# The delta projections of a selective scan, issued in pairs in the two row halves of TensorE

## The chip, the cores and the metric

The kernel runs on one core of a Trainium2 chip, as one launch. The metric is the device time of the whole launch in microseconds, lower is better. It was 7049.78 us in the median of three runs (7040.85 to 7054.37) before the change. All data is 32-bit floating point.

## What is computed

Two layers on an input of 2 images of 48 x 48 tokens with 768 channels, each added to its input:

```python
x = x + neighbourhood_attention(group_norm(x))     # 12 heads of 64, 7x7 neighbourhood
x = x + bidirectional_mamba(group_norm(x))
```

The second layer is where the change lies. For each image and each of two directions (the second on the reversed sequence, with weights of its own), over L = 2304 tokens and 1536 inner channels with 16 states:

```python
xz = in_proj(x);  u, z = split(xz)
u = silu(causal_depthwise_conv4(u))
dt, B, C = split(x_proj(u), [48, 16, 16])
delta = softplus(dt @ dt_proj_w.T + dt_proj_b)     # contraction over 48 (49 with the bias row)
h[t] = exp(delta[t] * A) * h[t-1] + delta[t] * u[t] * B[t]      # per channel and state
y[t] = sum over states of h[t] * C[t]  +  D * u[t]
out = out_proj((y_forward + y_backward) * silu(z))
```

The change touches the line that makes `delta`.

## The kernel before

**Tiling of the scan.** A direction of an image is cut into 6 chunks of 384 tokens (`CL`, `CHUNKS`), and the 1536 channels into 12 tiles of 128. One *unit* is one channel tile of one chunk; there are 2 x 2 x 6 x 12 = 288 of them, in a fixed order. For a unit, `scan` works in 4 groups of 4 states: `hb` is filled with `delta * u * B` (line 1254, on VectorE or GpSimd, whichever the planner picks for groups 1 to 3), ScalarE makes the decays `da = exp(delta * A)` (line 1276, one instruction per state), VectorE scans two states at a time (line 1287), GpSimd multiplies by `C` (line 1302), and TensorE adds the states up by transposing each 128-token piece into the accumulator `py` (line 1319). ScalarE then copies `py` out (line 1345). There are 7 `hb` buffers.

**Deltas.** `deltas_of` makes the deltas of three units (`KB = 3`, called a triple here) in one go, one triple ahead of the scan; 96 triples in all. SP fetches `u` (line 1166) and the 49 x 384 piece of the projection's weights and bias `dtw` (line 1167). For each of the three channel tiles, TensorE does one matmul of 49 rows by 128 columns by 384 tokens into an accumulator `mm` (line 1180), and ScalarE copies it into `dlt` (line 1186). One softplus over all three tiles follows, with an activation table load before and after it (lines 1191 and 1192). GpSimd then multiplies `u` by the delta (line 1204). The right-hand side `dt`, 49 x 384 with a row of ones, is fetched once per chunk (line 1399). A 32-bit matmul shows as two weight loads and two MATMUL records in the trace.

**Accumulators.** The tag `mm` has two buffers of one PSUM bank each. They serve nearly everything besides the scan's own `py` and `du`: the delta projections, the input, gate, state and output projections (all at line 387), the second image's attention, and the transposes that add the two directions (line 1372). `dtw`, `u` and `dlt` have two buffers each.

**Order of the work.** Nothing is issued where it is written down. Every piece of work is entered into `Order` with an engine, a price in ns, a key (the unit at which it is wanted) and the buffers it reads and writes. `Order.run` then simulates the engines with these prices and writes out one fixed sequence, in which each engine keeps its order. At each step it takes the work that can start first; among works of one engine that could start within 150 ns, the one with the smaller key (less a bonus, `early`). A work can only be taken when each buffer that it needs is free, which means that all works of the buffer's former holder have been placed. Works of the kind `job` (the projections and attention of later stages) may run at most 2.5 units ahead of the oldest unfinished work of the scan. Where TensorE would have more than 800 ns without work during a scan, transposes of the identity (line 1520) are put in as filler.

**Stages.** Up to about 1000 us the first image's attention runs alone. From then on the scan of the 288 units runs through to the end, and beside it, as jobs: the first image's projections, then (about 2750 to 3600 us) the second image's attention, then that image's projections and the output projections.

The change is in `deltas_of` (lines 1162 to 1188) and `chunk` (lines 1396 to 1401). The pricing functions are `mm(n, cl) = n * (cl * 1.69 + 5)` ns for n matmuls of cl columns, multiplied by 1.05 during the scan, and `act(n) = 60 + 0.833 n` ns.

Of the kernel before, what the change touches and what calls it, by code (L numbers as in the profile page):

```python
# [16 lines left out]
P = 128  # L17
# [23 lines left out]
NS = 16  # L41
RK = 48
XD = RK + 2 * NS
CL = 384
CHUNKS = [(l, CL) for l in range(0, L, CL)]
NCH = len(CHUNKS)
# [3 lines left out]
KB = 3  # L50
EARLY = 20
# [199 lines left out]
def tile_kernel(  # L251
# [3 lines left out]
    nc = tc.nc  # L255
# [14 lines left out]
    for i, (conv_w, conv_b, xpT, dtT, dt_b, A_log, Dp) in enumerate((fwd, bwd)):  # L270
        q = {"dtT": dram.tile([RK + 1, DI], F32, tag=f"dtT{i}", name=f"dtT{i}")}
# [17 lines left out]

    ones = wk.tile([1, CL], F32, tag="yt", name="ones", bufs=1)  # L290
    nc.gpsimd.memset(ones, 1.0)
# [12 lines left out]
    us = [spill(t, [DI, L], ND * NCW) for t in ("uf", "ub")]  # L304
    xd = [spill(t, [XD + 1, L], NCW) for t in ("xdf", "xdb")]
    sz = spill("sz", [DI, L], ND * NCW)
# [6 lines left out]
    def cols(l0, cl, k0=0, nk=1):  # L313

        c0, c1 = l0 // CW, (l0 + cl) // CW
        return [k * NCW + c for k in range(k0, k0 + nk) for c in range(c0, c1)]
# [7 lines left out]
    def sb(tag, shape, n, parts=1):  # L324
        return Buf(f"{tag}_{n}", wk, shape, tag, BUFS.get(tag, 1), parts)

    def ps(tag, n):
        return Buf(f"{tag}_{n}", psum, [P, 512], tag, BUFS.get(tag, 1))
# [5 lines left out]
    def add(eng, ns, fn, key, r=(), w=(), job=False, size=0, after=None, early=0, alt=None, due=False, opens=None):  # L334

        news = [x[0] if isinstance(x, tuple) else x for x in w]

        def issue():
            for v in news:
                if v.ap is None:  # L340
                    v.ap = v.pool.tile(v.shape, F32, tag=v.tag, name=v.name, bufs=v.bufs)
            fn()

        if eng == "PE":

            ns *= 1.04 if key < 0 else 1.05
        return order.add(eng, ns, issue, key, r, w, job, size, after, early, alt, due, opens)

    def mm(n, cl):
        return n * (cl * 1.69 + 5)  # L350

    def act(n, pointers=0):
        return 60 + 90 * pointers + n * 0.833
# [180 lines left out]
    def attention(b, start, end, job, T):  # L534
# [16 lines left out]
        def tag(what, i):  # L551
            return T[what][i % len(T[what])]
# [93 lines left out]
        def core(t):  # L646
# [12 lines left out]
            for g in range(NP // PG):  # L659
# [4 lines left out]
                kv = "v" not in T  # L664
                here = (2 * KB * CL - nk) // (PG * P) if kv else 0
                ks = sb(tag("k", g), [P, nk + here * PG * P], f"k{n}", parts=1 + here)
# [242 lines left out]
    def in_proj(b, i, start, end, conv=True, gate=True, nk=KB, tags=("uz",), banks=("mm",), proj=None):  # L909
# [3 lines left out]
        lo, n = l0 - HALO, cl + 2 * HALO  # L913
        xc = sb("xc", [P, NC, CL + 2 * HALO], f"{b}_{i}_{conv:d}{gate:d}", parts=NC)
        a, z = max(lo, 0), min(lo + n, L)
# [90 lines left out]
        for x, k0 in enumerate(range(0, ND, nk)):  # L1006
            if conv:
                uz = sb(tags[x % len(tags)], [P, 2, nk, CL], f"u{b}_{i}_{k0}", 2 * nk)
                for kk in range(nk):
# [6 lines left out]
            if gate and x % 2:  # L1016
                uz = sb(tags[x % len(tags)], [P, 1, 2 * nk, CL], f"z{b}_{i}_{k0}", 2 * nk)
                for kk in range(2 * nk):
# [3 lines left out]
    def staged(src, l0, cl, n, key, w=None, wsrc=None):  # L1022
# [3 lines left out]
        def fetch():  # L1026
# [5 lines left out]
            "SP", 800 if w else 400, fetch, key - 0.5, r=[(src, cols(l0, cl, 0, ND))],  # L1032
            w=[s, w] if w else [s], job=True, size=ND * P * (cl + (XD if w else 0)) * 4,
        )
        return s

    def x_proj_of(b, back, i, acc, key):

        n, (l0, cl) = f"{b}_{back}_{i}", CHUNKS[i]
        w = sb("xpw", [P, ND, XD], n)  # L1040
        add(
            "SP", 400, lambda: nc.sync.dma_start(w.ap, par[back]["xpT"]), key, w=[w], job=True,
            size=P * ND * XD * 4,
        )

        def take(uz, k0, nk, key):
            def part():
                for kk in range(nk):
                    nc.tensor.matmul(
                        acc[:XD, :cl], w[:, k0 + kk, :], uz[:, back, kk, :cl], start=k0 + kk == 0,  # L1050
                        stop=k0 + kk == ND - 1,
# [9 lines left out]
    def xd_out(b, back, l0, cl, n, acc, key):  # L1061
        t = sb("ev", [P, TB], n)
        add(
            "ACT", act(cl), lambda: nc.scalar.copy(t[:XD, :cl], acc[:XD, :cl]), key + 0.05, r=[acc],
            w=[t], job=True,
# [91 lines left out]
    def deltas_of(ch, k0, x):  # L1157

        q, b, back, l0, cl, dt = (ch[v] for v in ("q", "b", "back", "l0", "cl", "dt"))
        c, h, at, n = slice(0, cl), slice(1, cl + 1), x - 1.0, f"{ch['s']}_{k0}"  # L1160

        u, w = sb("u", [P, KB, CL + 2], n, KB), sb("dtw", [RK + 1, KB * P], n)
        dl = sb("dlt", [P, KB, CL], n, KB)

        def fetch():
            nc.sync.dma_start(u[:, :, h], rows_of(us[back][b], k0, KB, l0, cl))
            nc.sync.dma_start(w.ap, q["dtT"][:, k0 * P : (k0 + KB) * P])

        add(
            "SP", 800, fetch, at - 0.7, r=[(us[back][b], cols(l0, cl, k0, KB))], w=[u, w],  # L1170
            size=P * KB * (cl + RK) * 4,
        )
        add(
            "ACT", 100, lambda: nc.scalar.copy(u[:, :, :: cl + 1], one), at - 0.3, w=[u], early=EARLY,
        )
        for j in range(KB):
            acc = ps("mm", f"dl_{n}_{j}")
            add(
                "PE", mm(1, cl),
                lambda j=j, acc=acc: nc.tensor.matmul(  # L1180
                    acc[:, c], w[:, j * P : (j + 1) * P], dt[:, c], start=True, stop=True
                ),
                at + 0.01 * j, r=[dt, w, u], w=[acc, (dl, j)], early=EARLY,
            )
            add(
                "ACT", act(cl), lambda j=j, acc=acc: nc.scalar.copy(dl[:, j, c], acc[:, c]),  # L1186
                at + 0.01 * j, [acc], [(dl, j)], early=EARLY,
            )

        def softplus():  # L1190
            nc.scalar.activation(dl[:, :, c], dl[:, :, c], AF.Softplus)  # L1191
            nc.scalar.preload_act_table_set("natural_log_exp_and_others")  # L1192

        add("ACT", 2600 + 120 + act(KB * cl), softplus, at + 0.05, [dl], [dl], early=EARLY)
        vts = [sb("vt", [P, CL], f"{n}_{j}") for j in range(KB)]
        for j in range(KB):
            add(
                "ACT", act(cl, 1) + 40,
                lambda j=j: nc.scalar.mul(vts[j][:, c], u[:, j, h], q["Dp"][:, k0 + j : k0 + j + 1]),
                at + 0.03 + 0.25 * j, [(u, j)], [vts[j]], early=EARLY,  # L1200
            )
            add(
                "POOL", 960,
                lambda j=j: nc.gpsimd.tensor_mul(u[:, j, h], dl[:, j, c], u[:, j, h]), at + 0.06 + 0.25 * j,  # L1204
                [(dl, j), (u, j)], [(u, j)], early=EARLY,
            )
        return [((dl, j), (u, j), vts[j]) for j in range(KB)]
# [184 lines left out]
    def chunk(b, back, i, at):  # L1392

        l0, cl = CHUNKS[i]
        s = f"{b}_{back}_{i}"
        dt = sb("dt", [RK + 1, CL], s)
        src = xd[back][b]
        add(
            "SP", 400, lambda: nc.sync.dma_start(dt[:, :cl], src[: RK + 1, l0 : l0 + cl]), at - 1.4,
            [(src, cols(l0, cl))], [dt], size=RK * cl * 4,  # L1400
        )
        bc = []
        for g in (0, 1, 2, NSG, 3, NSG + 1, NSG + 2, NSG + 3):

            o = int(g < NSG)
            t = sb(f"bc{g}", [P, SG, CL + 2 * o], s, 1 + o)
            r = RK + 1 + g * SG
            add(
                "SP", 400,
                lambda t=t, r=r, o=o: nc.sync.dma_start(  # L1410
                    t[:, :, o : o + cl], src[r : r + SG, l0 : l0 + cl].partition_broadcast(P)
                ),
                at - 1 + 0.25 * (g % NSG) + 0.3 * (g >= NSG), [(src, cols(l0, cl))], [t],
                size=P * SG * cl * 4,
            )
            bc.append((g, t))
        bc = [t for g, t in sorted(bc, key=lambda x: x[0])]
        ends = (0, NCH - 1)

        ys = ()  # L1420
        if (b, back, i) == passes[-1]:
            parts = [sb(tag, [P, n, CL], f"y{tag}{n}", n) for tag, n in (("uz", 2 * KB), ("uz", KB), ("u", KB))]
            ys = [(y, k) for y in parts for k in range(y.parts)]
        return dict(
            q=par[back], b=b, back=back, l0=l0, cl=cl, dt=dt, bc=bc, s=s, i=i, ys=ys,
            first=i == ends[back], final=i == ends[not back],
        )
# [29 lines left out]
    for b in range(nb):  # L1457
        f = b * 2 * NCH * ND
        if b:
            attention(b, *A1, True, BESIDE)  # L1460
        for i in range(NCH):
            start = P1 + 12 * i if b else 9 * (i - 1) - 4
# [7 lines left out]
            else:  # L1470
                take, last = x_proj_of(b, 0, i, das[0], start - 1)
                in_proj(
                    b, i, start, end, gate=False, nk=2, tags=HEAD, banks=("mm", "mm", "py", "du"),
# [31 lines left out]
    for x, (p, b, back, i, k) in enumerate(units):  # L1505
# [6 lines left out]
        elif back and k == ND - 1:  # L1512
            for h, (l0, cl) in enumerate(PIECES[i]):
                at = x + 2.5 + 5 * h if b else 188 + 2 * (2 * (NCH - 1 - i) + h)
# [56 lines left out]
```

## Time and profile before

| | us |
|---|---|
| median of three runs | 7049.78 |
| the profiled execution | 7040.0 |
| its span, first to last instruction | 7038.2 |
| TensorE busy, matmuls (40140 records) | 6280.1 |
| VectorE busy | 5990.5 |
| GpSimd busy | 5468.5 |
| ScalarE busy | 4851.3 |

The groups of instructions that carry the scan and the deltas (count, total busy us, mean ns of one):

| line, engine, what | count | busy | mean |
|---|---|---|---|
| 1287 VectorE scan of two states | 2304 | 3923.6 | 1749 |
| 1302 GpSimd product with C | 1152 | 3652.7 | 3186 |
| 1276 ScalarE decay of one state | 4608 | 2677.4 | 584 |
| 1319 TensorE transposes into `py` | 13824 | 1750.0 | 279 |
| 1254 GpSimd filling of `hb` | 502 | 1606.8 | 3203 |
| 1254 VectorE filling of `hb` | 650 | 1131.3 | 1746 |
| 1186 ScalarE copy of a delta tile | 288 | 133.4 | 475 |
| 1180 TensorE weight loads of the deltas | 576 | 91.8 | 188 |

The time of one execution comes from the hardware profiler. Busy time is the union of an engine's instructions. The ends of TensorE's instructions are modelled and overlap the next ones, so for TensorE the distance between starts says more than the duration. A line of the page such as "DVE 1343..." gives the busy share of 40 equal slices of the span in tenths. After the bar, a group's line gives its total busy time, the mean of one in ns, the idle time of its engine just before it, and what ended that idle time.

### The profile page before, as it was taken

Reading aid. Unit: us, or ns where it says so; the run is one execution under the profiler, and the core shown is the slowest. Engines: PE = TensorE matmul, PEld = TensorE weight load, DVE = VectorE, ACT = ScalarE, POOL = GpSimd, SP = SyncE. Lnnn points to the kernel's source line nnn. Section 1 sums busy time; section 2 is a strip of 40 time slices with the busy share of each in tenths; the row PEclk is TensorE's granted clock in tenths of the full one; section 3 lists DMA queues with packets and bytes.
Section 4 is the critical chain, followed back from the end, with each engine's and each line's share of the span. In section 5 each row is a group of like instructions: output and inputs, shape, how many; then the busy total and the mean of one; then the engine's idle time right before and its main releaser. Section 6 shows DMA issues by size and latency. Waiting matters only on the chain. (4 is left out here: it accounts for less than half of the span.)

```text
span 7038.2 us, 108877 instructions
## 1 busy us (share of the span) xinstructions
PE 6280.1 (89%) x40140; PEld 4878.2 (69%) x40140; DVE 5990.5 (85%) x6102; ACT 4851.3 (69%) x10516; POOL 5468.5 (78%) x1958
## 2 busy tenths in 40 slices
PE   8999899899899989899988888888888898999888
PEld 5666656666667767666766666666678887777777
DVE  1343459999999989878899999999999999999998
ACT  1222248878887777677877777788876667777774
POOL 0000019898889989777889999999999999999997
PEclk9999999999999999999999999999999999999999
DMA  6666454544565455555542443343466676655553
GB/s 194 185 214 190 143 174 131 153 137 133 162 190 162 148 165 166 161 175 155 179 152 87 137 138 89 95 143 114 139 179 191 175 218 198 192 176 160 163 171 104
DMA packets 1348293, 1115.48 MB, mean 158 GB/s; under 512 B 137840, under 2 KB 1338000, under 8 KB 1347728
## 3 DMA queue, kind: packets, MB, share of 16 engines
q1 hardware_dynamic: 1347760, 1108.50, 52.6%
q8 instruction: 318, 5.21, 0.3%
q14 instruction: 215, 1.76, 0.1%
HBM read 895.34 MB, written 213.57 MB: 158 GB/s over the span
## 5 line engine op out<-in xcount | busy, mean ns | idle before, releaser
L1287 DVE TENSOR_TENSOR_SCAN hb<-da,hb 128x772 f32<-128x772 f32 x2304 | 3923.6, 1749 | 200.1 <-ACT da L1276 148.8
L1302 POOL TENSOR_TENSOR hb<-hb,bc 128x1536 f32<-128x1536 f32 x1152 | 3652.7, 3186 | 379.4 <-DVE hb L1287 287.9
L1276 ACT ACTIVATE da<-dlt,A 128x384 f32<-128x384 f32 x4608 | 2677.4, 584 | 962.5 <-DVE hb L1287 884.9
L1319 PE MATMUL py<-ident,hb 128*128 128x128 f32 x13824 | 1750.0, 279 | 313.5 <-POOL hb L1302 306.6
L1319 PEld LDWEIGHTS py<-ident,hb 128*128 128x128 f32 x13824 | 1566.1, 143 | 570.5 <-POOL hb L1302 471.7
L1254 POOL TENSOR_TENSOR hb<-u,bc 128x1544 f32<-128x1544 f32 x502 | 1606.8, 3203 | 48.7 <-PE py L1319 42.6
L1254 DVE TENSOR_TENSOR hb<-du,bc 128x1544 f32<-128x1544 f32 x650 | 1131.3, 1746 | 37.3 <-ACT du L1231 27.5
L1204 POOL TENSOR_TENSOR u<-dlt,u 128x384 f32<-128x384 f32 x288 | 263.6, 917 | 478.0 <-ACT dlt L1191 386.9
L1520 PE MATMUL py<-ident 128*128 128x128 f32 x5124 | 630.8, 277 | 0.0
L387 PE MATMUL mm_xin<-xc,w_x 128*128 128x390 f32 x1656 | 592.6, 501 | 29.8 <-DVE uz_u L964 12.6
L387 PE MATMUL mm_z<-xc,w_z 128*128 128x384 f32 x1728 | 607.6, 492 | 6.3 <-ACT dlt L1186 3.8
L1520 PEld LDWEIGHTS py<-ident 128*128 128x128 f32 x5124 | 586.8, 143 | 17.3 <-issue 13.6
L387 PE MATMUL mm_out<-stage_y,w_o 128*128 128x192 f32 x3168 | 558.0, 330 | 18.9 <-DMA w_o<-in_w_opT 6.5
L387 PEld LDWEIGHTS mm_out<-stage_y,w_o 128*128 128x128 f32 x3168 | 519.0, 193 | 30.5 <-ACT dlt L1186 10.6
L930 POOL MEMSET xc<- 128x18 f32 x4 | 0.5, 118 | 630.0 <-PE mm_v L387 630.0
L964 DVE SCALAR_TENSOR_TENSOR uz_u<-mm_xin,conv_w,uz_u 128x384 f32<-128x384 f32 x792 | 427.9, 610 | 45.6 <-ACT uz_u L957 44.0
L387 PEld LDWEIGHTS mm_xin<-xc,w_x 128*128 128x128 f32 x1656 | 306.3, 193 | 230.2 <-issue 28.8
L387 PE MATMUL mm_qk<-xc_xn,w_qk 128*128 128x384 f32 x1296 | 452.8, 495 | 8.7 <-DVE sm L794 2.6
L387 PEld LDWEIGHTS mm_z<-xc,w_z 128*128 128x128 f32 x1728 | 314.8, 192 | 192.4 <-issue 9.4
L387 PEld LDWEIGHTS mm_qk<-xc_xn,w_qk 128*128 128x128 f32 x1296 | 238.6, 192 | 161.8 <-issue 15.9
L1260 ACT COPY bc<-state 128x8 f32<-128x8 f32 x960 | 183.0, 196 | 143.9 <-DVE hb L1254 68.3
L800 ACT ACTIVATE pr<-pr,sm 128x196 f32<-128x196 f32 x432 | 194.0, 450 | 126.4 <-DVE sm L794 124.8
(163 smaller groups left out, 6454.8 us busy)
## 6 DMA issues: line engine op xcount, KB each, us to landing
w_o<-in_w_opT SPq DMA_DIRECT2D x264, 384.0 KB
bc<-xdf SPq DMA_DIRECT2D x96, 768.0 KB
bc<-xdb SPq DMA_DIRECT2D x96, 768.0 KB
w_qk<-in_w_qkv SPq DMA_DIRECT2D x144, 384.0 KB
w_x<-in_w_inT SPq DMA_DIRECT2D x144, 384.0 KB
w_z<-in_w_inT SPq DMA_DIRECT2D x144, 384.0 KB
w_ao<-in_w_out SPq DMA_DIRECT2D x72, 384.0 KB
u<-uf SPq DMA_DIRECT2D x48, 576.0 KB
```

The source lines that it names most:

```text
L387: nc.tensor.matmul(acc[:m, o0 : o0 + cl], wb[:, wi, wo : wo + m], xb[:, xi, xo : xo + cl], start=c == 0, stop=c == n - 1,)
L800: nc.scalar.activation(pr[:, v, :], pr[:, v, :], AF.Exp, bias=sm[:, v : v + 1], scale=-1.0, accum_out=sm[:, UU + v : UU + v + 1],)
L930: nc.gpsimd.memset(xc[:, :, : a - lo], 0.0)
L964: nc.vector.scalar_tensor_tensor(u, px[:, at[j] : at[j] + cl], q["conv_w"][:, k, j : j + 1], u, ALU.mult, ALU.add,)
L1204: lambda j=j: nc.gpsimd.tensor_mul(u[:, j, h], dl[:, j, c], u[:, j, h]), at + 0.06 + 0.25 * j,
L1254: on.tensor_mul(cells(hb, SG), by.unsqueeze(1).to_broadcast([P, SG, W]), bc[g].ap)
L1260: "ACT", 98, lambda: nc.scalar.copy(bc[g][:, :, ends], was), now - 0.4,
L1276: lambda: nc.scalar.activation(cells(da, 2)[:, j % 2, h], dl[:, jd, c], AF.Exp, scale=q["A"][:, k, i : i + 1]),
L1287: lambda: nc.vector.tensor_tensor_scan(flip(hb[at2]), flip(da[:, : 2 * W]), flip(hb[at2]), 0.0, ALU.mult, ALU.add),
L1302: lambda: nc.gpsimd.tensor_mul(cells(hb, SG)[:, :, h], cells(hb, SG)[:, :, h], bc[NSG + g][:, :, c]),
L1319: nc.tensor.matmul(py[:tp, t * P : (t + 1) * P], cells(hb, SG)[:, j, h][:, tb[t]], ident, start=False, stop=g == NSG - 1 and j == SG - 1 a ...
L1520: nc.tensor.matmul(marks["py"][:, CL : CL + P], ident, ident, start=False, stop=False, is_transpose=True, skip_group_check=True,)
```

## The change

The weights `dtw` and the right-hand side `dt` are put into SBUF twice: in partitions 0 to 48, and again in partitions 64 to 112. `dtw` and `dt` therefore have 113 partitions instead of 49, with as many bytes per partition as before, and each is loaded by two DMAs instead of one. The three channel tiles of a triple are taken as a pair and a single one. The two matmuls of the pair are one piece of work for the planner; the first reads the lower copy, the second the upper one, and each writes an `mm` accumulator of its own, so the pair needs both. The third tile reads the lower copy. The prices change: the pair costs 1.6 times one matmul, the single one 1.2 times, and the load of `dt` is entered with twice the time and the bytes; the entry for the fetch of `u` and `dtw` keeps its price and size. The copies, the softplus and everything behind are as before.

```diff
--- before.py
+++ after.py
@@ -41,6 +41,7 @@
 NS = 16
 RK = 48
 XD = RK + 2 * NS
+ROW = 64
 CL = 384
 CHUNKS = [(l, CL) for l in range(0, L, CL)]
 NCH = len(CHUNKS)
@@ -1159,12 +1160,13 @@
         q, b, back, l0, cl, dt = (ch[v] for v in ("q", "b", "back", "l0", "cl", "dt"))
         c, h, at, n = slice(0, cl), slice(1, cl + 1), x - 1.0, f"{ch['s']}_{k0}"
 
-        u, w = sb("u", [P, KB, CL + 2], n, KB), sb("dtw", [RK + 1, KB * P], n)
+        u, w = sb("u", [P, KB, CL + 2], n, KB), sb("dtw", [ROW + RK + 1, KB * P], n)
         dl = sb("dlt", [P, KB, CL], n, KB)
 
         def fetch():
             nc.sync.dma_start(u[:, :, h], rows_of(us[back][b], k0, KB, l0, cl))
-            nc.sync.dma_start(w.ap, q["dtT"][:, k0 * P : (k0 + KB) * P])
+            for r in (0, ROW):
+                nc.sync.dma_start(w[r : r + RK + 1], q["dtT"][:, k0 * P : (k0 + KB) * P])
 
         add(
             "SP", 800, fetch, at - 0.7, r=[(us[back][b], cols(l0, cl, k0, KB))], w=[u, w],
@@ -1173,19 +1175,26 @@
         add(
             "ACT", 100, lambda: nc.scalar.copy(u[:, :, :: cl + 1], one), at - 0.3, w=[u], early=EARLY,
         )
-        for j in range(KB):
-            acc = ps("mm", f"dl_{n}_{j}")
-            add(
-                "PE", mm(1, cl),
-                lambda j=j, acc=acc: nc.tensor.matmul(
-                    acc[:, c], w[:, j * P : (j + 1) * P], dt[:, c], start=True, stop=True
-                ),
-                at + 0.01 * j, r=[dt, w, u], w=[acc, (dl, j)], early=EARLY,
-            )
-            add(
-                "ACT", act(cl), lambda j=j, acc=acc: nc.scalar.copy(dl[:, j, c], acc[:, c]),
-                at + 0.01 * j, [acc], [(dl, j)], early=EARLY,
-            )
+        for j0 in range(0, KB, 2):
+            js = range(j0, min(j0 + 2, KB))
+            accs = [ps("mm", f"dl_{n}_{j}") for j in js]
+
+            def raw(js=js, accs=accs):
+                for j, acc in zip(js, accs):
+                    r = slice(j % 2 * ROW, j % 2 * ROW + RK + 1)
+                    nc.tensor.matmul(
+                        acc[:, c], w[r, j * P : (j + 1) * P], dt[r, c], start=True, stop=True
+                    )
+
+            add(
+                "PE", mm(1, cl) * (1.6 if len(js) > 1 else 1.2), raw, at + 0.01 * j0, r=[dt, w, u],
+                w=[*accs, *((dl, j) for j in js)], early=EARLY,
+            )
+            for j, acc in zip(js, accs):
+                add(
+                    "ACT", act(cl), lambda j=j, acc=acc: nc.scalar.copy(dl[:, j, c], acc[:, c]),
+                    at + 0.01 * j, [acc], [(dl, j)], early=EARLY,
+                )
 
         def softplus():
             nc.scalar.activation(dl[:, :, c], dl[:, :, c], AF.Softplus)
@@ -1393,12 +1402,14 @@
 
         l0, cl = CHUNKS[i]
         s = f"{b}_{back}_{i}"
-        dt = sb("dt", [RK + 1, CL], s)
+        dt = sb("dt", [ROW + RK + 1, CL], s)
         src = xd[back][b]
-        add(
-            "SP", 400, lambda: nc.sync.dma_start(dt[:, :cl], src[: RK + 1, l0 : l0 + cl]), at - 1.4,
-            [(src, cols(l0, cl))], [dt], size=RK * cl * 4,
-        )
+
+        def rows():
+            for r in (0, ROW):
+                nc.sync.dma_start(dt[r : r + RK + 1, :cl], src[: RK + 1, l0 : l0 + cl])
+
+        add("SP", 800, rows, at - 1.4, [(src, cols(l0, cl))], [dt], size=2 * RK * cl * 4)
         bc = []
         for g in (0, 1, 2, NSG, 3, NSG + 1, NSG + 2, NSG + 3):
```

## The prediction

> **What bounds the kernel now.** I read the page's busy shares and tenths first, then a table of the engines by stretch, then the chain of waits, and only then the instructions that change.
>
> ```profile
> span 7038.2 us, 108877 instructions
> PE 6280.1 (89%) x40140; PEld 4878.2 (69%) x40140; DVE 5990.5 (85%) x6102; ACT 4851.3 (69%) x10516; POOL 5468.5 (78%) x1958
> ...
> DVE  1343459999999989878899999999999999999998
> ...
> POOL 0000019898889989777889999999999999999997
> ...
> DVE 18%; POOL 5%; issue 5%; ACT 4%; PE 3%; DMA 1%; DVEq 0%; SPq 0%; POOLq 0%
> ```
>
> PE has the largest total, but not the bound: from the sixth slice on VectorE and GpSimd stand at nine tenths, and the chain that ended last (it covers 36% of the span, all late) is half VectorE and only 3 parts in 36, some 8%, TensorE. The table by stretch (columns: PE, PEld, DVE, ACT, POOL busy, clock, DMA share, GB/s) says where this differs.
>
> ```profile
> 1000.00:2000.00 1000.00, 909.67 (x4759) 648.47 (x4758) 918.75 (x791) 808.27 (x1550) 876.21 (x313) 0.98 0.48 144
> 2750.00:3500.00 750.00, 683.23 (x5070) 513.86 (x5069) 616.20 (x731) 571.89 (x1476) 580.96 (x208) 0.97 0.56 174
> 3750.00:4750.00 1000.00, 846.27 (x5572) 677.11 (x5571) 973.87 (x804) 772.59 (x1515) 959.18 (x340) 0.98 0.38 117
> 6000.00:7000.00 1000.00, 896.08 (x5821) 750.45 (x5820) 971.01 (x669) 746.34 (x1571) 955.20 (x341) 0.99 0.56 166
> ```
>
> Only 2750 to 3500, where the second image's attention runs beside the scan, has TensorE at 91% with VectorE at 82% and GpSimd at 77%. In the last two stretches both scan engines are at 96 to 97%. And much of TensorE's time there is filler, the identity transposes of line 1520:
>
> ```profile
> L1520 PE MATMUL py<-ident 128*128 128x128 f32 x5124 | 630.8, 277 | 0.0
> ...
> L1180 PE MATMUL mm_dl<-dt,dtw 49*128 49x384 f32 x576 | 245.7, 531 | 34.7 <-ACT dlt L1186 11.1 <-DVE xr L1108 5.8 <-DMA dtw<-dtT 5.6
> ```
>
> The delta projections are 288 matmuls, two records each; mean durations overlap their neighbours, so I use start to start. The timeline of TensorE at one triple, and two lines from the attention scores (16 and 8 records), which already use both row halves:
>
> ```profile
> 4017.45 2.15 PE L387 MATMUL mm_xin<-xc,w_x 128*128 128x390 f32 x6
> 4019.53 0.91 PE L1180 MATMUL mm_dl<-dt,dtw 49*128 49x384 f32 x2
> 4020.37 0.55 PE L1335 MATMUL py<-ident,vt 128*128 128x128 f32 x3
> 4020.75 2.13 PE L387 MATMUL mm_xin<-xc,w_x 128*128 128x390 f32 x6
> ...
> 4029.47 1.55 PE L1180 MATMUL mm_dl<-dt,dtw 49*128 49x384 f32 x4
> 4030.95 0.33 PE L1520 MATMUL py<-ident 128*128 128x128 f32 x1
> ```
>
> ```profile
> 2967.74 0.88 PE L784 MATMUL mm_s<-uz_k,xpw_q 64*64 64x196 f32 x8
> ...
> 2989.87 1.54 PE L784 MATMUL mm_s<-uz_k,xpw_q 64*64 64x196 f32 x16
> ```
>
> A lone tile blocks TensorE for 0.84 us (4019.53 to 4020.37), two together for 1.48 (4029.47 to 4030.95): 0.64 for a tile, 0.2 for coming and going. The first tile of this triple stands 10 us before the other two, between two input products that use the same two accumulators.
>
> **What the Trainium skill says.** "TensorEngine Tiling (Array Packing)", Key Properties: tiles work independently, and a change of tiling mode drains the array. The trace agrees. Eight more records of 196 columns cost 1.54 - 0.88 = 0.66 us in the scores; serially, at the 0.32 us that a 384-column record takes here, they would cost 8 x 0.163 = 1.31. And the 0.2 us is paid before the change too, so its mode changes are not new. The same page, Gotcha 1: different row tiles may not use one PSUM bank at a time; the change gives each half its own `mm` buffer. Its section PSUM Bottleneck: tiling speeds the array, not the evacuation; here the ScalarE copies stay 288 of 474 ns.
>
> **TensorE's part.** Per triple: before, three slots of 0.64; after, a pair in one slot and the third tile in another. If the halves overlap as in the scores, 0.64 us less per triple, 96 x 0.64 = 61 us. Bounds: 0 if they run serially, 61 if fully; scores split the columns too, which the projections do not, so that is the unproven part. I take 61. How much arrives? In 2750 to 3500 lie 66/6 = 11 triples (66 of the records fall in it): 11 x 0.64 = 7 us, taken whole, because TensorE leads there. The other 85 triples save 54 us, of which I let through the 8% that TensorE has of the chain: 4 us. The rest becomes filler or idle time under the scan. At the first triple (projections 1008.0 to 1011.4, first decay activation 1017.3) nothing hides the projection: about 1 us. Sum: -12, bounds 0 and -61.
>
> **The pair's two accumulators.** Before, a tile went as soon as one of two `mm` buffers was free; now the pair needs both emptied, and the third tile waits for the pair's first copy. In 59 of 96 triples the second tile started over 1.6 us after the first, which two free buffers would not need. How late may it be? The median from softplus to the first decay activation of the triple is 38 us (one triple: projections 4091.6, softplus 4098.8, first use 4137.5). I followed each buffer from its first matmul to its last reader: the time from a triple's first projection until the other users had left both buffers is 0 to 1.4 us in the median and 15.5 at most. So late deltas are covered; without the cover each us late would stop both scan engines. Not covered is what queues behind: TensorE executes in order, and while the pair waits for a slower evacuation, the transposes behind it (line 1319) wait, which hold the `hb` buffers that VectorE and GpSimd fill next. Now 34.7 us of idle stand before the projections. Bounds: 0 (the plan puts the pair where both are free) to 96 x 1.3 us (one more copy latency per triple) = 125 us of TensorE time, at 8% 10 us, at 30% 37. I take 4.
>
> **DMAs.** 96 more weight loads of 73.5 KB at 0.39 us of SP each, and 24 more `dt` loads: 47 us on a queue whose issues in the trace add up to 2141 us, 8.8 MB on 1115. SP's next works (loads of `zs`, `yl` and weights) shift by 0.4 us a triple. Cover: from issue to first projection is 13 us in the triple above (4078.5 to 4091.6), and projections waited for these weights 6 us in all. Cost 0 to 3 us, I take 1. The plan prices the fetch at 800 as before, so it runs 0.4 us optimistic.
>
> **The plan itself.** The order is computed from priced works. The triple's price goes from 3 x 687 to 1098 + 824 ns, and the buffer rule is stricter, so later choices move too, such as who fills `hb` (now GpSimd 502, VectorE 650). This has no sign. Size: VectorE's scans wait 200 us in all, GpSimd's products 379; a tenth more or less of one of them is 20 to 38 us. I take 0, keeping +-30.
>
> **Sum.** -12 + 4 + 1 = -7 against the profiled 7040.0 us (span 7038.2 and 1.8 around it). With the bank cost at its lower end it is -12. The median of the three runs shown lies 9.8 us above the profiled execution, and the sum is carried over to it. As the plan's price per lone tile (now 824 against some 840 seen; before 687) is nearer to what happens, I lean to the lower end: -12, from the median 7050 to 7038.
>
> **Rivals.**
> *A, relief with a similar order (0.44): 7038*, own range 7018 to 7053. For: the scores' overlap, the 38 us cover. Against: TensorE isn't the bound in most stretches.
> *B, the two-buffer wait becomes the bound (0.37): 7074.* One mechanism: TensorE stands before the pair until the later of two evacuations, and the transposes behind it free `hb` late. Place: 1000 to 2000 and 3750 to 4750, where by my count both buffers were free only 9% and 6% of the time. Price: 96 x 1.3 us = 125, and 30% of it reaching the scan, less 12: +25. It decides once more than about 10% of that standing reaches the scan. Against it: filler of 55 us and more per 250 us in the second of these stretches.
> *C, the new order happens to pack VectorE and GpSimd better (0.14): 7010.* Relief 12 and a tenth of the 288 us that GpSimd's products wait for scans. Nothing in the profile speaks for its sign.
> *D, the halves run one after the other (0.05): 7053.* Then only waits and DMAs remain, +3. Against: the scores.
>
> **Numbers.** A measurement of this kernel tells about 0.2% (14 us) from no change: the three runs span 13.5 us. Of A, 0.27 lies below 7036 and 0.17 inside; of B, 0.35 above 7064 and 0.02 inside; C is faster; D is inside but for 0.01. Faster 0.41, same 0.23, slower 0.36. Range for 8 in 10: from C's 7008 to 7084, somewhat past B's centre.
>
> **What would show it.** A pair of tiles starting within a few ns, four records in about 0.84 us: the relief is right; 1.48 refutes it. Filler (630.8) should rise by some 20 to 50 us. Idle before the projections (34.7) staying under 60 speaks for A, over 100 for B, with more idle before the transposes and `hb` fills. The stretch of the second attention should end about 7 us earlier. The median from softplus to first use falling from 38 below 15 us, or scans waiting for `da` much beyond 149 us, would make the cover wrong. A changed split of fills with shifted waits of VectorE and GpSimd, while the projections behave, says that the order decided and not the arrays.

## The result: 12 us slower, and the profile after

The changed kernel takes 7062.07 us in the median of 14 runs (7050.49 to 7076.25), beside 7049.84 us in 14 runs of the kernel before (7040.85 to 7059.39). The ratio of the changed kernel's time to that before is 1.0018 with a 95% interval of 1.0011 to 1.0025: inside the 0.2% that the prediction called no change, but outside chance, and on the other side from the forecast of 7038.

The page of the changed kernel: the busy totals, the chain of waits by engine, and the groups to compare; the second block has three of these groups in the kernel before.

```profile
span 7067.2 us, 109208 instructions
...
PE 6279.6 (89%) x40197; PEld 4876.7 (69%) x40197; DVE 5995.5 (85%) x6106; ACT 4850.4 (69%) x10516; POOL 5457.3 (77%) x1954
...
DVE 40%; PE 20%; ACT 13%; POOL 10%; issue 9%; DMA 6%; SPq 2%; DVEq 0%; POOLq 0%; ACTq 0%
...
L1296 DVE TENSOR_TENSOR_SCAN hb<-da,hb 128x772 f32<-128x772 f32 x2304 | 3920.6, 1748 | 171.5 <-ACT da L1285 140.2
L1311 POOL TENSOR_TENSOR hb<-hb,bc 128x1536 f32<-128x1536 f32 x1152 | 3655.0, 3188 | 388.1 <-DVE hb L1296 312.1
...
L1263 DVE TENSOR_TENSOR hb<-du,bc 128x1544 f32<-128x1544 f32 x654 | 1137.6, 1746 | 73.3 <-ACT du L1240 52.1
...
L1531 PE MATMUL py<-ident 128*128 128x128 f32 x5181 | 635.9, 277 | 0.0
```

```profile
L1287 DVE TENSOR_TENSOR_SCAN hb<-da,hb 128x772 f32<-128x772 f32 x2304 | 3923.6, 1749 | 200.1 <-ACT da L1276 148.8
L1302 POOL TENSOR_TENSOR hb<-hb,bc 128x1536 f32<-128x1536 f32 x1152 | 3652.7, 3186 | 379.4 <-DVE hb L1287 287.9
...
L1254 DVE TENSOR_TENSOR hb<-du,bc 128x1544 f32<-128x1544 f32 x650 | 1131.3, 1746 | 37.3 <-ACT du L1231 27.5
```

No single line explains the loss. TensorE's total is the same within 1 us although its projections became cheaper, and the filler (now line 1531) rose by 5 us only. VectorE's scans wait 29 us less, but its fillings of `hb` wait 36 us more, and GpSimd's products 9 us more. GpSimd now fills `hb` 498 times instead of 502, VectorE 654 times instead of 650. The chain reaches back over the whole span this time, so its shares can't be set against those of the shorter chain before.

The groups of the projections (now line 1185), and the waits around them:

```profile
L1185 PE MATMUL mm_dl<-dt,dtw 49*128 49x384 f32 x576 | 215.1, 557 | 59.7 <-ACT dlt L1195 21.2 <-DVE xr L1109 18.7 <-DMA dtw<-dtT 9.2
```

```profile
its engine sat idle before it (us, times) until:
  ACT dlt L1195: 53.8, 55
  DVE xr L1109: 45.3, 37
```

Busy time fell from 245.7 to 215.1 us, idle before it rose from 34.7 to 59.7. The idle time of TensorE's matmuls and weight loads together that ended with VectorE emptying an accumulator of the output projection (`DVE xr`) went from

```profile
  DVE xr L1108: 15.5, 15
```

to the 45.3 above.

**Two tiles that start together overlap completely, but fewer than half of the pairs do.** TensorE's timeline at a pair, in the changed kernel:

```profile
1163.50 0.92 PE L1185 MATMUL mm_dl<-dt,dtw 49*128 49x384 f32 x4
1164.35 0.55 PE L1344 MATMUL py<-ident,vt 128*128 128x128 f32 x3
```

Four records, and the next instruction starts 0.85 us after the first; a lone tile took 0.84. The same place in an execution with the same order, but both tiles in the lower rows (`e5_loads_serial` below):

```profile
1149.60 1.55 PE L1185 MATMUL mm_dl<-dt,dtw 49*128 49x384 f32 x4
1151.08 0.55 PE L1344 MATMUL py<-ident,vt 128*128 128x128 f32 x3
```

1.48 us, so such a pair saves about the predicted 0.64 us. But the two tiles start within 10 ns of each other in only 44 of the 96 pairs. In 18 more the second tile follows within 0.4 us and overlaps in part, and in 34 it starts later, up to 5.2 us, and little or nothing overlaps. One of these 34:

```profile
5978.15 0.91 PE L1185 MATMUL mm_dl<-dt,dtw 49*128 49x384 f32 x2
5979.30 0.91 PE L1185 MATMUL mm_dl<-dt,dtw 49*128 49x384 f32 x2 [0.24 <-DVE xr L1109]
5980.14 1.53 PE L1328 MATMUL py<-ident,hb 128*128 128x128 f32 x12
```

The planner takes the pair as one piece of work that needs both accumulators. On the chip each matmul waits for its own accumulator alone: here the first starts, and the second stands until VectorE has emptied the other one. In 27 of the 34 late pairs the trace names VectorE or ScalarE, emptying an accumulator, as what the second tile waited for. What the overlap saves in all can be read from `e5_loads_serial` and `a_again`, a second profile of the changed kernel, which have the same order:

```profile
L1185 PE MATMUL mm_dl<-dt,dtw 49*128 49x384 f32 x576 | 250.2, 536 | 51.9 <-DVE xr L1109 17.5 <-ACT dlt L1195 13.3 <-DMA dtw<-dtT 5.3
```

```profile
L1185 PE MATMUL mm_dl<-dt,dtw 49*128 49x384 f32 x576 | 214.6, 555 | 59.5 <-ACT dlt L1195 20.8 <-DVE xr L1109 17.7 <-DMA dtw<-dtT 9.3
```

The projections keep TensorE busy for 36 us less, not 61. Most of the additional standing is there in `e5` too, without any overlap (51.9 us).

**Not all 29 us between the two profiles belong to the change.** The profiled execution before took 7040.0 us, 10 less than the median of its kernel, and the one of the changed kernel 7069.04, 7 more. The order of every engine is the same in both kernels until the first triple's weights are fetched at about 950 us, and TensorE's until after 1015 us. Yet in the table by stretch (length, TensorE's busy time and records, granted clock, DMA share, GB/s) the kernel before has

```profile
800.00:850.00 50.00, 43.13 (x326) 0.97 0.62 189
```

and the changed one

```profile
800.00:850.00 50.00, 43.93 (x240) 0.76 0.55 161
```

The granted clock differed in that execution, and fewer records fell into those 50 us. At the end of the first unit the changed kernel is 7.3 us late, of which this is likely a part; the second profile of it (`a_again`) is 3.7 us late there and ends 6 us earlier. The medians, 12 us apart, are the safer number.

### The profile page after: what moved, and what is told of

Read it like the earlier page. It is cut to its first block, busy times and chain, and to the rows that moved or that the text cites. A ratio compares the mean times of both kernels' runs of the same rounds, so it can differ in the third digit from the quotient of the medians.

```text
span 7067.2 us, 109208 instructions
## 1 busy us (share of the span) xinstructions
PE 6279.6 (89%) x40197; PEld 4876.7 (69%) x40197; DVE 5995.5 (85%) x6106; ACT 4850.4 (69%) x10516; POOL 5457.3 (77%) x1954
## 4 chain that ended last, share of the span: by engine, by line
DVE 40%; PE 20%; ACT 13%; POOL 10%; issue 9%; DMA 6%; SPq 2%; DVEq 0%; POOLq 0%; ACTq 0%
DVE hb L1296 27%; DVE hb L1263 7%; POOL hb L1311 7%; PE mm_qk L388 5%; ACT da L1285 4%; DVE uz_u L965 4%; POOL hb L1263 2%; PE py L1328 2%; PE mm_ao L388 2%; PE mm_v L388 2%; PE mm_xin L388 1%; SPq L752 1%; DMA bc_v<-vd 1%; PE da L785 1%; ACT uz_u L958 1%
## 5 line engine op out<-in xcount | busy, mean ns | idle before, releaser
L1531 PE MATMUL py<-ident 128*128 128x128 f32 x5181 | 635.9, 277 | 0.0
L388 PE MATMUL mm_out<-stage_y,w_o 128*128 128x192 f32 x3168 | 554.5, 328 | 10.2 <-DVE xr L1109 2.7
```

The source lines that it names most:

```text
L388: nc.tensor.matmul(acc[:m, o0 : o0 + cl], wb[:, wi, wo : wo + m], xb[:, xi, xo : xo + cl], start=c == 0, stop=c == n - 1,)
L1531: nc.tensor.matmul(marks["py"][:, CL : CL + P], ident, ident, start=False, stop=False, is_transpose=True, skip_group_check=True,)
```

## The experiments

The change has two sides. It alters what the chip does (doubled loads, row halves), and it alters what the planner is told (a pair that needs two accumulators, other prices of the projections, and a load of `dt` entered at twice its price), from which a new order follows on all engines. The experiments take the sides apart. A ratio is always to the kernel before on the same chip.

### Old order, new hardware work

```diff
 # in the kernel before; prices, keys and buffers untouched
-acc[:, c], w[:, j * P : (j + 1) * P], dt[:, c], start=True, stop=True
+acc[:, c], w[j % 2 * ROW : j % 2 * ROW + RK + 1, j * P : (j + 1) * P],
+dt[j % 2 * ROW : j % 2 * ROW + RK + 1, c], start=True, stop=True
 # and both loads doubled as in the change
```

> The plan of the kernel before (same prices, three separate projections), but with dt and its weights loaded twice and the second tile's matmul reading the upper copy, so that it can overlap where it stands next to the first. If the recomputed order made the change slower: same as before, ratio 0.998 to 1.0005. If the doubled loads or the row halves cost the time: 1.001 to 1.0025, like the changed kernel.

Measured: 7049.59 us, ratio 0.9998 (0.9991 to 1.0004). The order of every engine is that of before; the projections' busy time fell to 210.4 us, as neighbouring tiles lie in different halves and overlap here too. So 120 extra loads and 35 us less of TensorE together are worth nothing that can be measured in that order. Three separate projections, without any rule that pairs them, relieve TensorE as much as the pair does.

### New order, old hardware work

```diff
 # e2: in the changed kernel
-for r in (0, ROW):                                  # both loads
+for r in (0,):
-r = slice(j % 2 * ROW, j % 2 * ROW + RK + 1)
+r = slice(0, RK + 1)
 # e5: only the second edit, loads stay doubled
```

> The plan of the changed kernel, instruction for instruction, but single loads and all projections in the lower rows, so the pair runs serially. If the order costs the time: 1.001 to 1.003, no better than the changed kernel. If loads or halves cost it: 0.999 to 1.0005. If the overlap is worth the 61 us of TensorE that the prediction counted at some 10%, it is about 6 to 10 us above the changed kernel.

> The changed kernel once more, beside e2_again and e5_loads_serial on the same chip. It should repeat 1.001 to 1.0025.

> The order of the changed kernel with single loads and all projections in the lower rows, once more. If the overlap is worth some 17 us in this order, as the first run of it and the changed kernel suggest: 0.002 to 0.003 above a_again. If the overlap is worth nearly nothing, as in the old order: within 0.0008 of a_again, and the first run of it stood too high.

> The order of the changed kernel and its doubled loads, but both tiles of the pair read the lower copy and run one after the other. If the doubled loads cost nothing: equal to e2_again within 0.0008. If they cost the 47 us of SP and more: 0.001 or more above it. Against a_again it is the price of the overlap alone: 0.0000 to 0.0008 if hidden, 0.002 or more if it reaches the end.

| | ratio | interval |
|---|---|---|
| `e2_new_order` | 1.0042 | 1.0029 to 1.0054 |
| `a_again`, the changed kernel | 1.0026 | 1.0017 to 1.0035 |
| `e2_again` | 1.0038 | 1.0025 to 1.0051 |
| `e5_loads_serial` | 1.0042 | 1.0028 to 1.0055 |

In each of these runs every engine keeps the order of the changed kernel. That order alone costs some 0.4%, about 28 us (7054 x 0.004). The doubled loads add 0.0004, within the intervals. The overlap takes back 0.0012 to 0.0016 in the runs on the same chip, some 8 to 11 us; the intervals overlap, so this part is likely but not shown. It lies between the two outcomes that were stated for `e2_again`, and between the two for `e5` against `a_again`; `e2` came out above its stated 1.001 to 1.003 and `a_again` just above its 1.0025.

How far each kernel has come at the same unit shows this better than the totals. From each profile I took the end of ScalarE's copy out of `py` (line 1345 before), once for each unit; the table has the time before and the difference to it in us. Each column is one execution: that of before is 10 us faster than its median, and that of `e5` took 7058 us, by far the fastest of its five (median 7083), so shapes count here, not the last row.

| unit | before | e1, old order | changed | a_again | e2, its order | e5, its order | g1 | f4 | g2 |
|---|---|---|---|---|---|---|---|---|---|
| 0 | 1053.3 | 3.4 | 7.3 | 3.7 | 1.0 | -6.6 | -3.0 | 4.6 | 0.3 |
| 72 | 2588.7 | 0.2 | 1.1 | -2.0 | -2.2 | -10.6 | -14.0 | -6.0 | -10.4 |
| 96 | 3168.7 | 3.1 | 3.6 | 3.5 | 7.2 | -2.7 | -33.1 | -27.8 | -29.4 |
| 120 | 3720.3 | 0.4 | 15.2 | 16.2 | 22.7 | 14.2 | -35.4 | -28.0 | -28.4 |
| 144 | 4237.1 | 0.5 | 7.4 | 8.4 | 15.0 | 5.8 | -28.7 | -21.6 | -22.2 |
| 180 | 4971.4 | 0.2 | 12.2 | 16.2 | 27.7 | 10.2 | -12.0 | -6.6 | -8.3 |
| 216 | 5669.7 | 0.2 | 21.2 | 17.4 | 31.1 | 12.1 | -12.3 | -12.9 | -13.4 |
| 287 | 7007.5 | 2.3 | 22.9 | 16.5 | 31.5 | 12.0 | -12.2 | -10.5 | -11.1 |

Kernels with the same order gain and lose in the same places whatever their loads and rows: `e1` stays within 4 us of before all the way, and the four with the new order lose most of their time in the same two places, units 72 to 120 (the second image's attention and the first input projections after it, 14 to 25 us) and units 144 to 216 (6 to 16 us). In the first of them, two of the longest waits between 2750 and 3500 us, by engine and line (total us, times, longest), were in the kernel before

```profile
POOL hb L1302 <- DVE hb L1287: 68.0, 36, 8.9
DVE pr L794 <- PE mm_s L784: 20.6, 12, 9.0
```

and in the second profile of the changed kernel

```profile
POOL hb L1311 <- DVE hb L1296: 90.5, 41, 11.6
DVE pr L795 <- PE mm_s L785: 31.2, 17, 8.2
```

GpSimd's products stand 22 us longer for VectorE's scans, and the attention's masks 11 us longer for their scores. Which placement makes them wait was not traced further.

### Which part of the planning?

First, two of the three planning edits apart. The third, the higher price of `dt`'s load, stays in both kernels:

```diff
 # e3: in the changed kernel, the projections' prices of before
-"PE", mm(1, cl) * (1.6 if len(js) > 1 else 1.2), raw, ...
+"PE", mm(1, cl) * (2 if len(js) > 1 else 1), raw, ...
 # e4: in e1_old_order, three separate works, new prices, and dt's load priced as in the change
-"PE", mm(1, cl),
+"PE", mm(1, cl) * (1.2 if j == KB - 1 else 0.8),
```

> The changed kernel with the prices of before (pair 2, single 1 matmul), so the pair's need of both accumulators is left and the new prices are gone. If the two-accumulator rule costs the time: 1.001 to 1.003. If the prices do: 0.999 to 1.0005. If any change of plan moves the time by chance: anything from 0.997 to 1.005, and unlike the changed kernel.

> Three separate projections (one accumulator each) with the new prices spread over them (0.8, 0.8, 1.2 matmul), the doubled loads and the row halves as in the change. If the two-accumulator rule costs the time: 0.998 to 1.0005. If the prices do: 1.001 to 1.003. If any change of plan moves the time by chance: anything from 0.997 to 1.005, with no relation to e3.

Measured: `e3` 1.0043 (1.0031 to 1.0056), `e4` 1.0011 (1.0004 to 1.0017). Either edit, with the load's price, is already slower than before, and the pair at the old prices is slower than the whole change. The two don't add up, and of the stated outcomes the last, that any change of plan moves the time, fits both best. The load's price was never changed alone; it is not told apart from the others. To see how much any change of order does, I changed one price in the kernel before, with nothing of the change in it:

```diff
-"PE", mm(1, cl),
+"PE", mm(1, cl) * 1.05,      # p1; p2: 0.95, p5: 1.22
```

> The kernel before with one number changed: the planner's price of a delta projection times 1.05. Loads, rows and accumulators are as before. If only the change's own rule (the pair needs both accumulators) costs the time: same, within 0.9995 to 1.0005. If the order before is simply a favourable one and any other is worse: 1.001 to 1.005. If orders scatter evenly about it: anywhere in 0.996 to 1.004.

> The same with the price times 0.95. Pair rule alone: 0.9995 to 1.0005. Order before a favourable one: 1.001 to 1.005. Even scatter: anywhere in 0.996 to 1.004, without relation to p1_price_up.

> The kernel before with a projection priced 1.22 times, which is the 0.84 us that a lone tile was seen to block TensorE for (0.687 before). If truer prices make a better order: 0.997 to 0.9995. If the order before is a favourable one: 1.001 to 1.005.

and in the changed kernel the prices of the pair and of the third tile to what a pair that overlaps was seen to take, and both of its prices by 5%:

```diff
-"PE", mm(1, cl) * (1.6 if len(js) > 1 else 1.2), raw, ...
+"PE", mm(1, cl) * 1.28, raw, ...                            # p4
+"PE", mm(1, cl) * (1.68 if len(js) > 1 else 1.26), raw, ... # e6
```

> The changed kernel with pair and third tile both priced 1.28 matmul, near what the trace of the changed kernel shows for a pair that overlaps. If the change lost because its pair was priced too high (1.6): 0.998 to 1.001. If the two-accumulator rule costs the time whatever the price, or any new order does: 1.001 to 1.005.

> The changed kernel with its two prices 5% higher (1.68 and 1.26). If the pair's need of two accumulators has a cost of its own: 1.0015 to 1.0045, above all plans with separate projections. If orders only scatter: anything in 0.999 to 1.0045, under 1.001 as likely as not.

Then two more with the pair and two with separate works, all with the doubled loads and the row halves:

```diff
+"PE", mm(1, cl) * (2.1 if len(js) > 1 else 1.05), raw, ...  # f1; f2: 1.9 and 0.95
+"PE", mm(1, cl) * 1.1,                                      # f3, separate; f4: 0.9
```

> The changed kernel with the pair priced 2.1 and the third tile 1.05. If the rule of two accumulators has its own cost: 1.002 to 1.0045. If orders only scatter: 0.999 to 1.002.

> The changed kernel with the pair priced 1.9 and the third tile 0.95. If the rule of two accumulators has its own cost: 1.002 to 1.0045. If orders only scatter: 0.999 to 1.002.

> Three separate projections priced 1.1, with the doubled loads and the row halves of the change. If the rule of two accumulators is the cost: 0.999 to 1.0015. If any other order than the old one costs the same: 1.002 to 1.004.

> Three separate projections priced 0.9, with the doubled loads and the row halves of the change. If the rule of two accumulators is the cost: 0.999 to 1.0015. If any other order than the old one costs the same: 1.002 to 1.004.

| order with | kernel: ratio (interval) |
|---|---|
| the pair, both accumulators at once | `f1` 0.9997 (0.9989 to 1.0005), `p4` 1.0010 (1.0002 to 1.0018), the change 1.0018 (1.0011 to 1.0025), `f2` 1.0028 (1.0017 to 1.0040), `e6` 1.0029 (1.0018 to 1.0041), `e3` 1.0043 (1.0031 to 1.0056) |
| separate projections | `f4` 0.9960 (0.9947 to 0.9972), `p1` 0.9993 (0.9985 to 1.0001), `f3` 0.9998 (0.9988 to 1.0008), `p2` 1.0011 (1.0004 to 1.0017), `e4` 1.0011 (1.0004 to 1.0017), `p5` 1.0014 (1.0008 to 1.0020) |

A price moved by 5 to 22%, in work that takes about 4% of TensorE's busy time, shifts the whole kernel with separate projections by anything from -28 us (`f4`; -17 us without the row halves, `g1` below) to +10 us. `f4` lies outside both outcomes that were stated for it; of the pairs, `f1` fell where scatter was expected and `f2` where a cost of the rule was, and `e6` fits both. `p1` fits only the even scatter, `p2` also a favourable old order, `p5` only that, and `p4` lies on the border of its two. Truer prices gave no order better than before: `p5` and `p4` price what the traces show and are slower than that. Among the pairs, though, `p4` is faster than `e3`, which has the prices of before. The two groups differ in the mean (1.0021 and 0.9998) but overlap, and `f1`, with the full rule, is as fast as before. All of the pairs also carry the higher price of `dt`'s load, of the others only `e4`. So a cost of the rule of its own is possible but not shown; that the order decides is.

Nor is the wait for `DVE xr` a mark of the rule. It is 45.3 us in the change, 33.7 in `f1` and 17.5 in `e4`, but only 15.1 in `p4`, whose pair needs both accumulators, and 23 in `f3` and `p1`, which have no pair. It goes with the order as well.

### The fast order, with and without the halves

```diff
 # g1: in the kernel before, nothing else
-"PE", mm(1, cl),
+"PE", mm(1, cl) * 0.9,
```

> The kernel before with a projection priced 0.9: the order of f4_single_down, with single loads and all projections in the lower rows. If f4 is fast by its order: 0.995 to 0.9975. If by the overlap: 0.999 to 1.001.

> f4_single_down once more on the same chip: 0.9945 to 0.9975. The overlap and the doubled loads together are worth its difference from g1: within 0.001 if TensorE's saved time is hidden in this order too.

Measured: `g1` 7036.72 us, 0.9976 (0.9967 to 0.9986); `g2`, which is `f4` again, 7030.76 us, 0.9968 (0.9956 to 0.9981). Both beat the kernel before and the changed one. The order of `f4` explains most of its gain, without any of the change; the halves and loads add 0.0008, some 6 us, within the intervals. In the table by unit, `g1`, `f4` and `g2` go together: 19 to 22 us won between units 72 and 96, and more than half of their lead lost again later. That stretch by engine (PE, PEld, DVE, ACT, POOL busy, clock, DMA share, GB/s), first in `a_again`, then in `f4`:

```profile
2750.00:3500.00 750.00, 671.53 (x5020) 507.56 (x5020) 608.40 (x726) 564.21 (x1464) 570.62 (x204) 0.97 0.57 173
```

```profile
2750.00:3500.00 750.00, 686.70 (x5096) 515.82 (x5095) 626.01 (x742) 576.59 (x1492) 596.60 (x212) 0.98 0.57 173
```

In the same 750 us, at the same rate of transfers, `f4` keeps every engine busier, GpSimd by 26 us. It is not that one engine has less to do; all of them stand less. The window is the same in time, not in work, so this says that `f4` gets more done there, and not which wait it avoids.

## Why the prediction was wrong, point by point

- **TensorE's part** ("I take 61"; 12 us of it to arrive). The mechanism is right where it applies: 0.85 us for a pair against 1.48, in full-width matmuls too. The size is not: only 44 of 96 pairs start together, and TensorE is relieved of 36 us. What the end of the kernel got of them was 1 to 2 us in the old order, some 6 in that of `f4`, and 8 to 11 in the changed one, none of them clear of the noise. The 12 is the upper end, near it partly by luck, as a smaller relief met a larger share that arrives. That the 0.2 us of coming and going is the change of mode was assumed; no run here takes it apart.
- **"The rest becomes filler"**: expected +20 to 50 us, seen +5 (635.9) and -3 (`a_again`, 627.8). The filler is written into the plan: 5181 transposes in all four kernels with the new order, with the overlap or without. Time that is saved only on the chip can't turn into filler; it went into longer standing.
- **The pair's two accumulators** ("I take 4"). The cover held: the median from softplus to the first decay is about 36 us after, 38 before. The standing is there, 59.7 us of idle beside 34.7, just under the 60 that the prediction set as the border of case A. But in the 34 late pairs TensorE does not wait before the pair for the later accumulator; it waits between the two tiles, which costs the overlap. What the standing costs at the end can't be told from the cost of the order.
- **DMAs** ("0 to 3 us, I take 1"): `e5` against `e2_again` gives +3 us (0.0004), inside the noise. Right as far as it can be seen.
- **The plan itself** ("This has no sign", "I take 0, keeping +-30"). This is the step that failed. The new order costs about 28 us with the old hardware work, the upper end of that band. With 8 to 11 us taken back by the overlap, the change is slower by the 12 us of the first measurement or the 18 us of `a_again`. That a new order could outweigh everything else in the sum stood in the prediction as its size, and still entered the sum as zero. The split of the `hb` fills and the shifted waits of VectorE and GpSimd are the sign that the prediction had named for this case. Which placements in the new order cost the time stays open.
- **The second attention** should have ended about 7 us earlier; its last matmul ends 12 to 14 us later (3624.8 before, 3639.2 and 3636.8 after), in the first of the two places where the order loses.
- **The lean** ("As the plan's price per lone tile ... is nearer to what happens, I lean to the lower end"): not borne out. With the lone tile's price made true (`p5`) the kernel is slower than before. The lean also drops two costs: with the accumulators at 0 and the loads at 1, the sum is -11, not -12.
- **Rival B** named +25 by TensorE standing before the pair. The standing exists, but only 25 us more of it, and an order with the rule (`f1`) costs nothing. It was near in the number for a reason that the runs do not carry.

## What to carry to other kernels

Where a planner writes the order, a change has to be tested twice: with the old order kept (only the hardware work changes) and with the new order on the old work. Otherwise the scatter of orders, here -0.4 to +0.4%, is read as the merit of an optimization that is worth less than that. And since a one-number edit of a price found -0.24% (`g1`, the best of those tried) where packing the array found at most 0.16%, it pays to try several orders for the same work before changing the work. Where two matmuls are to overlap, count in the trace how many pairs start together, and don't judge by one of them.

## What was not expected of the hardware

Two 49-row, 128-column, 384-token matmuls in the two row halves overlapped fully where they started together, although they share all columns, which the scores in the kernel before did not: their first records start some 10 ns apart and the pair takes the 0.85 us of one tile. The prediction had counted on it without proof. What it did not expect is that 52 of the 96 pairs don't start together, mostly because each matmul waits for its own accumulator. And the granted clock differed between two executions that were still in the same sequence of instructions: 0.97 and 0.76 in the same 50 us of the first stage, with 326 and 240 records of TensorE.
